# Which side of a trip through memory is cut in four: the store of the transposed probabilities, or the load

## The chip, the cores and the metric

The kernel runs on one core of one Trainium2 chip. The metric is device time in microseconds (us), the median over several executions. A profile of one execution shows its engines: PE (TensorE matrix products; PEld is its weight load), DVE (VectorE), ACT (ScalarE), POOL (GpSimd) and SP (SyncE, which here only issues transfers). Transfers (DMAs) issued by SP and ACT run on the same sixteen DMA engines.

## The reference, cut to what matters

Eight sequences of 512 rows of 256 numbers (float32) go through causal attention with 16 query heads in 4 groups, and then through a mixture of 64 experts with a shared expert. What matters here is the attention of one head:

```
scores = q @ k.T / sqrt(128)          # 512 x 512, query t by key s
scores = where(s <= t, scores, -inf)
probs  = softmax(scores, axis=-1)
out    = probs @ v                    # sum over keys s
```

The softmax is taken along the keys, so a row of probabilities has its query in the partition. The product with v sums over the keys, so TensorE wants the keys in the partition: each head's probabilities have to be transposed between the two.

## The kernel before, in words

There are 8 x 16 = 128 heads, numbered k, and one long loop over them (L944). The order of the instructions on each engine is written out by hand (`manual_schedule`, L135). An iteration k does, in this order:

- `scores(k, 0)` and `scores(k, 1)`: products of q and k, a DVE reduction that adds the mask and finds the maximum (L293), and the exponential on ACT (L296);
- `turned(k - 1)` (L312): the transposition of the head before;
- `scores(k, 2)` and `scores(k, 3)`; `weigh(k)`, in which POOL multiplies by the reciprocal sums (L306);
- `project(k - 3)`, `queries(k + 1)`, and `mix(k - 2)` (L343), which multiplies the transposed probabilities `et` with v (L349).

So what `turned(k)` makes in iteration k + 1 is used in iteration k + 2, after that iteration's scores, projection and queries.

`turned` works in two steps, because DVE's transpose works inside blocks of 32 x 32. First, six DVE transposes (L322) turn the blocks in place, into `eb`, which holds, for partition p, four chunks c (which block of 32 keys inside a tile of 128), each with ten blocks of 32 numbers (only the tiles on and below the diagonal). After that, partition p = 32 a + s of `eb` holds, in chunk c, numbers that belong in partition 32 c + s of `et`, chunk a. This exchange of the block index a with c goes through memory. `ex_d` is a scratch tensor in memory of 128 rows by 4 x 320 numbers, of which there are two, used in turn. One transfer stores `eb` to it as it is, 128 rows of 5,120 bytes (L326). Four transfers then load `et`, one for each 32 partitions c of it: each takes from 128 rows of `ex_d` a piece of 1,280 bytes (L329). All five are issued by SP, which takes its instructions strictly in order; the loads wait for the landing of the store. Each head has its own such trip, except the last two (126 and 127), which TensorE transposes (`turned_at_once`, L332).

There is one buffer `eb` (`bufs=1`, L314), so DVE's transposes of the next head wait until the store has read it. There are two buffers `et`, so the load for head k waits until `mix(k - 2)` is done.

Other transfers on SP stand around these: loads of the next sequence's rows `x`, stores of rows for the feed-forward part, and, late in the loop, the result. From about head 97 on the expert part runs inside the same loop: ACT issues three loads of 352 KB for each of 32 pairs of experts (L523, L530), between its exponentials, and POOL gathers and scatters rows. All transfers of SP and ACT use eight completion semaphores in turn, in the order of the program, and a transfer is issued only when the one eight places ahead of it has landed.

Of the kernel before, what the change touches and what calls it, by code (L numbers as in the profile page):

```python
# [22 lines left out]
NI = T // P  # L23
BS = 32
# [20 lines left out]
def sandwich_kernel(ctx, tc, x, wq, bq_t, wkv, bk_t, bv, wo, gate_wt, w_gate, w_up, w_down,  # L45
                    sh_gate_t, sh_up_t, sh_down_t, pe_t, out):
    nc = tc.nc
# [75 lines left out]
    with ExitStack() as part:  # L123
# [38 lines left out]
        for half, (t, w) in enumerate(((sg_sb, sh_gate_t), (su_sb, sh_up_t))):  # L162
            nc.sync.dma_start(out=t[:, :, :FSH], in_=w.rearrange("(c p) n -> p c n", p=P))
            nc.sync.dma_start(out=t[:, :, FSH:],
                              in_=gate_wt.rearrange("(c p) n -> p c n", p=P)[:, :, ts(half, NX // 2)])
# [146 lines left out]
        def turned(k):  # L312
            l = live[k]
            eb = p2.tile([P, NI, NB, BS], F32, tag="eb", name=f"eb_{k}", bufs=1)  # L314
            for i in range(NI):
                for js in ([0, 1], [2, 3]):
                    js = [j for j in js if j <= i]
                    if not js:
                        continue
                    at, step = AT[js[0]] + i - js[0], AT[js[-1]] - AT[js[0]] - 1  # L320
                    blocks = eb[:, :, at : at + step * (len(js) - 1) + 1 : max(step, 1), :]
                    nc.vector.transpose(  # L322
                        blocks.rearrange("p c j t -> p j c t"),
                        l["e"][i][:, js[0] * P : (js[-1] + 1) * P].rearrange("p (j c t) -> p j c t", c=NI, t=BS))
            ex = ex_d[k % 2]
            nc.sync.dma_start(out=ex, in_=eb.rearrange("p c n t -> p c (n t)"))  # L326
            l["et"] = p2.tile([P, NI, NB, BS], F32, tag="et", name=f"et_{k}")
            for c in range(NI):
                nc.sync.dma_start(out=l["et"][ts(c, BS)].rearrange("s a n t -> s a (n t)"),  # L329
                                  in_=ex[:, c, :].rearrange("(a s) f -> s a f", s=BS))  # L330

        def turned_at_once(k):  # L332

# [610 lines left out]
        for k in range(NK):  # L944
            b, s = divmod(k, NH)
# [3 lines left out]
            if 0 <= k - 1 < NK - 2:  # L949
                turned(k - 1)  # L950
# [141 lines left out]
```

## Time and profile before

| what | value |
|---|---|
| three runs | 1455.51, 1459.09, 1459.84 us; median 1459.09 |
| the profiled execution, its own time | 1456.37 us |
| span of its core | 1454.6 us, mean granted TensorE clock 0.987 |
| PE busy | 1403.1 us, 96% of the span |
| DVE, ACT, POOL busy | 892.8, 505.8, 429.2 us |
| DMA moved | 252.03 MB, mean 173 GB/s |
| issues `ex_d<-eb` (L326) | 126, 640 KB each |
| issues `et<-ex_d` (L329) | 504, 160 KB each |

The span runs from the core's first to its last instruction; the execution's own time is 1.8 us more. Busy time is a share of the span over all stages; what counts at a place is which wait ends last there. In the 40 slices of the span, a digit 9 is 90% or more. A group of instructions shows its busy time, the mean of one, and, after the bar, how long its engine stood idle just before and for what. In the list of waits, a line says which engine at which line waited for what, the sum in us, the number of waits and the longest. "SPq" is SP's queue, which is not counted as busy.

### The profile page before, as it was taken

To read this page: it belongs to the slowest core of one execution; us is meant where nothing else is said; L and a number is where in the kernel's file an instruction comes from. 1 tells how busy PE (TensorE), PEld (TensorE's weight loads), DVE (VectorE), ACT (ScalarE), POOL (GpSimd) and SP (SyncE) were. 2 spreads that over 40 slices of the span, in tenths; PEclk is the share of its full clock that TensorE was granted. 3 is DMA by queue.
4 is the path that set the end of the run, shared out by engine and by line. 5 is a ranking of instruction groups with operands and counts; after the bars stand their busy time and mean duration, and the time that the engine had idled before them with its cause. 6 is when DMAs were issued, how large, how long until landed. Compare 5 with 4: busy or idle time off the path is not lost. (4 is left out here: it accounts for less than half of the span.)

```text
span 1454.6 us, 18553 instructions
## 1 busy us (share of the span) xinstructions
PE 1403.1 (96%) x5310; PEld 855.2 (59%) x5310; DVE 892.8 (61%) x3097; ACT 505.8 (35%) x1442; POOL 429.2 (30%) x686
## 2 busy tenths in 40 slices
PE   9999999999999999999999999999989999999895
PEld 5665665656556665666566665655545655556563
DVE  5565576656765577557665676576455454567634
ACT  2333343234422333234323442233433243434431
POOL 2222232123211231124211321125434444344511
PEclk9999999999999999999999999999999999999998
DMA  7664464355544554445534554449999889878812
GB/s 258 195 201 141 144 181 146 95 156 167 164 128 128 163 174 128 122 145 182 155 109 139 165 173 128 123 139 264 258 261 234 230 241 260 220 196 235 248 53 81
DMA packets 160790, 252.03 MB, mean 173 GB/s; under 512 B 16412, under 2 KB 136189, under 8 KB 160685
## 3 DMA queue, kind: packets, MB, share of 16 engines
q1 hardware_dynamic: 125869, 201.52, 46.5%
q10 hardware_dynamic: 28672, 39.85, 9.9%
q0 software_dynamic: 6144, 9.44, 3.4%
q8 instruction: 44, 0.72, 0.2%
q14 instruction: 61, 0.50, 0.1%
HBM read 143.01 MB, written 107.74 MB: 172 GB/s over the span
## 5 line engine op out<-in xcount | busy, mean ns | idle before, releaser
L306 POOL TENSOR_SCALAR e<-e,recip 128x128 f32<-128x128 f32 x508 | 274.1, 597 | 787.0 <-DVE recip L303 749.1
L296 ACT ACTIVATE e<-e,least 128x128 f32<-128x128 f32 (+3 forms) x512 | 285.8, 559 | 377.5 <-DVE least L293 338.9
L289 PE MATMUL psc<-kt,qt 128*128 128x128 f32 (+3 forms) x1024 | 310.0, 442 | 13.9 <-DVE qt L279 6.7
L349 PE MATMUL pav<-et,v 128*128 128x512 f32 (+3 forms) x1024 | 300.0, 436 | 5.0 <-DMA et<-ex_d 3.4
L349 PEld LDWEIGHTS pav<-et,v 128*128 128x128 f32 x1024 | 194.9, 192 | 166.8 <-issue 122.6
L293 DVE CUSTOM_DVE_ANT_0 e<-psc,mask 128x128 f32<-128x128 f32 (+3 forms) x512 | 232.7, 479 | 74.9 <-PE psc L289 67.5
L361 PE MATMUL po<-wo_sb,ao 128*128 128x256 f32 x1024 | 243.5, 381 | 0.7 <-ACT ao L109 0.7
L276 PE MATMUL pq<-xnt,wq_sb 128*128 128x512 f32 x512 | 242.1, 595 | 0.0
L361 PEld LDWEIGHTS po<-wo_sb,ao 128*128 128x128 f32 x1024 | 193.0, 190 | 72.3 <-issue 40.7
L322 DVE STREAM_TRANSPOSE eb<-e 128x128 f32<-128x128 f32 x756 | 228.1, 365 | 8.6 <-DMA ex_d<-eb 6.4
L109 ACT COPY ao<-pav 128x512 f32<-128x512 f32 x128 | 74.9, 585 | 427.4 <-PE pav L349 406.7
L289 PEld LDWEIGHTS psc<-kt,qt 128*128 128x128 f32 x1024 | 167.9, 192 | 90.7 <-issue 22.2
L279 DVE SCALAR_TENSOR_TENSOR qt<-pq,bq_sb,pe_sb 128x512 f32<-128x512 f32 x128 | 95.5, 746 | 93.5 <-PE pq L276 93.3
L276 PEld LDWEIGHTS pq<-xnt,wq_sb 128*128 128x128 f32 x512 | 96.3, 191 | 69.7 <-issue 64.2
L303 DVE RECIPROCAL recip<-total 128x4 f32<-128x4 f32 x128 | 22.8, 178 | 121.6 <-ACT e L296 120.6
L296 ACT ACTIVATION_READ_ACCUMULATOR e<-e,least 128x1 f32 x512 | 95.8, 187 | 0.0
L586 POOL DMA_INDIRECT y_d<-dd,idx x32 | 51.2, 1600 | 130.3 <-DMA y_d<-dd,idx 85.6
L248 PE MATMUL pk<-xnt,wkv_sb 128*128 128x512 f32 x128 | 60.3, 594 | 0.2 <-ACT xnt L109 0.2
L261 DVE TENSOR_TENSOR v<-pv,bv_sb 128x512 f32<-128x512 f32 x32 | 22.1, 691 | 60.8 <-PE pv L259 60.8
L259 PE MATMUL pv<-wkv_sb,xnt 128*128 128x512 f32 x128 | 59.1, 593 | 0.0
L112 DVE COPY ht<-pth 88x256 f32<-88x256 f32 x32 | 13.4, 418 | 67.8 <-PE pth L566 52.9
L251 DVE SCALAR_TENSOR_TENSOR kt<-pk,bk_sb,pe_sb 128x512 f32<-128x512 f32 x32 | 24.0, 750 | 47.4 <-PE pk L248 47.4
(197 smaller groups left out, 1118.2 us busy)
## 6 DMA issues: line engine op xcount, KB each, us to landing
ex_d<-eb SPq DMA_DIRECT2D x126, 640.0 KB
et<-ex_d SPq DMA_DIRECT2D x504, 160.0 KB
wgu<-in_w_gate ACTq DMA_DIRECT2D x32, 352.0 KB
wgu<-in_w_up ACTq DMA_DIRECT2D x32, 352.0 KB
wd<-in_w_down ACTq DMA_DIRECT2D x32, 352.0 KB
y<-y_d ACTq DMA_DIRECT2D x10, 512.0 KB
x<-in_x SPq DMA_DIRECT2D x8, 512.0 KB
x_d<-x SPq DMA_DIRECT2D x8, 512.0 KB
```

What stands on the lines that cost most here:

```text
L109: nc.scalar.copy(dst, src)
L248: nc.tensor.matmul(pk, lhsT=wkv_sb[:, c, g, 0, :], rhs=s["xnt"][:, c, :], start=c == 0, stop=c == NC - 1)
L259: nc.tensor.matmul(pv, lhsT=s["xnt"][:, c, ts(i, P)], rhs=wkv_sb[:, c, :, 1, :], start=c == 0, stop=c == NC - 1)
L276: nc.tensor.matmul(pq, lhsT=wq_sb[h // QPG][:, c, ts(h % QPG, D)], rhs=seqs[b]["xnt"][:, c, :], start=c == 0, stop=c == NC - 1)
L279: nc.vector.scalar_tensor_tensor(qt, pq, bq_sb[:, h : h + 1], pe_sb, ALU.add, ALU.add)
L289: nc.tensor.matmul(psc[:, :w], lhsT=l["qt"][:, ts(i, P)], rhs=seqs[b]["kt"][h // QPG][:, :w], start=True, stop=True)
L293: nc.vector.tensor_tensor_reduce(out=e, in0=psc[:, :w], in1=mask[:, T - w :], scale=-1.0 / math.sqrt(D), scalar=BIG, op0=ALU.add, op1=ALU. ...
L296: nc.scalar.activation(e, e, AF.Exp, bias=l["least"][:, i : i + 1], scale=-1.0, accum_out=l["total"][:, i : i + 1])
L306: engine.tensor_scalar(e, e, recip[:, n : n + 1], 1.0, ALU.mult, ALU.mult)
L322: nc.vector.transpose(blocks.rearrange("p c j t -> p j c t"), l["e"][i][:, js[0] * P : (js[-1] + 1) * P].rearrange("p (j c t) -> p j c t", ...
L349: nc.tensor.matmul(pav[:, :, j:, :], lhsT=seqs[b]["v"][:, j, ts(g, D)], rhs=l["et"][:, :, AT[j] : AT[j] + NI - j, :], start=j == 0, stop=j ...
L361: nc.tensor.matmul(po[b][i // 2][:, i % 2, :], lhsT=ao[:, ts(i, P)], rhs=wo_sb[:, h, :], start=h == 0 and i % 2 == 0, stop=h == NH - 1, sk ...
```

## The change

The store is cut in four and the load is made whole. For each a, the 32 partitions 32 a to 32 a + 31 of `eb` are stored by one transfer; chunk c of partition 32 a + s goes, as a piece of 1,280 bytes, to row 32 c + s of `ex_d`, place a. So `ex_d` has the rows of the partitions of `et`, and one transfer loads them: 128 rows of 5,120 bytes. The bytes are the same, and there are five transfers as before, all on SP, in the same place of the program. The order of instructions on DVE, ACT, POOL and PE is the same; the semaphore waits around the transfers differ, and so does the place of some ACT loads between SP's transfers in the common order of the eight semaphores.

```diff
             ex = ex_d[k % 2]
-            nc.sync.dma_start(out=ex, in_=eb.rearrange("p c n t -> p c (n t)"))
+            for a in range(NI):
+                nc.sync.dma_start(out=ex[:, a, :].rearrange("(c s) f -> s c f", s=BS),
+                                  in_=eb[ts(a, BS)].rearrange("s c n t -> s c (n t)"))
             l["et"] = p2.tile([P, NI, NB, BS], F32, tag="et", name=f"et_{k}")
-            for c in range(NI):
-                nc.sync.dma_start(out=l["et"][ts(c, BS)].rearrange("s a n t -> s a (n t)"),
-                                  in_=ex[:, c, :].rearrange("(a s) f -> s a f", s=BS))
+            nc.sync.dma_start(out=l["et"].rearrange("s a n t -> s (a n t)"), in_=ex.rearrange("p a f -> p (a f)"))
```

## The prediction

> **What bounds the kernel now.** First the page's slices: who is busy, and where.
>
> ```profile
> PE   9999999999999999999999999999989999999895
> PEclk9999999999999999999999999999999999999998
> DMA  7664464355544554445534554449999889878812
> ```
>
> PE is full from start to end, while the DMA engines are half idle up to slice 27 and full behind it. A table by stage, with sum of PE in each, says how much is to be won:
>
> ```profile
> 27.00:980.00 953.00, 945.01 (x3295) 578.77 (x3294) 612.13 (x2129) 331.01 (x972) 232.83 (x429) 1.00 0.50 150
> 1000.00:1280.00 280.00, 269.04 (x1261) 156.16 (x1260) 152.01 (x523) 99.36 (x272) 124.61 (x142) 0.98 0.94 241
> 1280.00:1400.00 120.00, 109.13 (x420) 70.06 (x419) 77.79 (x273) 50.76 (x136) 48.14 (x70) 0.96 0.72 209
> ```
>
> Columns: stretch, its length, PE busy first, then the other engines, at the end the clock, the DMA share and GB/s. PE idles 8 us in 953 of the quiet stage, 11 in 280 of the expert stage, 11 in 120 of the tail. Now what of this the trip through memory causes: the groups that read `et` and write `eb`, and the waits of SP.
>
> ```profile
> L349 PE MATMUL pav<-et,v 128*128 128x512 f32 (+3 forms) x1024 | 300.0, 436 | 5.0 <-DMA et<-ex_d 3.4
> L322 DVE STREAM_TRANSPOSE eb<-e 128x128 f32<-128x128 f32 x756 | 228.1, 365 | 8.6 <-DMA ex_d<-eb 6.4
> SPq L326 <- DVE eb L322: 457.9, 105, 9.8
> SPq L329 <- DMA ex_d<-eb: 427.1, 125, 10.8
> ```
>
> PE stands 5.0 us before these 1024 products, 3.4 of it one wait for `et`; DVE stands 6.4 us for `eb` to be free. SP's 427 us for the store cost nothing as long as `et` is in time. So the trip is nearly all hidden, and the question is how near it is to showing. A quiet head on SP:
>
> ```profile
> 608.58 0.34 SPq L326 DMA_DIRECT2D ex_d<-eb  x1
> 611.58 1.73 SPq L329 DMA_DIRECT2D et<-ex_d  x4
> ```
>
> 3.00 us from store issue to first load issue. The trace's semaphore updates and packets give the rest (medians of 64 quiet heads). Store: first packet 0.84 us after issue, last packet ended at 2.59, landed at 2.94; its 128 packets of 5,120 bytes take 199 ns each, eight per engine, 1.59 us. Loads: issued 0.43 apart, so the fourth at 1.30; packets from 0.93 to 4.16, landed at 4.88; their 512 packets of 1,280 bytes take 84 ns in the mean, though the shortest take 53. Round trip 2.94 + 0.06 + 4.88 = 7.88 us. From landing to the first product of that head there are 4.0 us in the median of heads 0 to 79, at least 0.14; above 2 us in nearly all. From store landing to DVE's next transpose: mostly above 2.5 us, least 0.8 in the quiet stage.
>
> The only places where it shows are in the expert stage at 1049 and 1184 (PE gaps of 1.28 and 0.32 us before `pav`) and here, in the chain that ended last:
>
> ```profile
> 1356.31 5.21 DMA out_dram<-x
> 1361.54 0.38 SPq L670
> 1362.02 7.22 DMA ex_d<-eb
> 1370.63 3.63 DMA et<-ex_d
> 1374.39 4.60 PE pav L349 x8
> ```
>
> Head 124's store waits behind a result and an `x` load on SP, then shares the DMA with 1.5 MB of others, and PE waits 3.40 us for `et` at 1374.
>
> [...] Here the smallest undisturbed store, 128 KB of zeros at 24.81 us, landed after 1.97 us[...].
>
> **The change part by part.**
>
> *Removed:* one store (2.94 us to landing) and four loads (4.88). SP issue 0.34 + 4 x 0.43 = 2.1 us.
>
> *Added, the four stores.* The last is issued at 1.30 us. [...] 1.30 + 0.84 + eight packets of 55 ns (0.44) + 0.35 receipt = 2.93. If it is limited as the loads were (packets over 3.23 us): 0.84 + 3.23 + 0.35 = 4.42; with the loads' slower landing 4.88. I take 4.4[...]. A gain below 2.93 is excluded by the issue spacing.
>
> *Added, the one load.* 0.93 + 1.75 (the store's packet span[...]) + the loads' landing lag of 0.72 = 3.4; at worst 4.88 as now. The wait before it is for four or five semaphores instead of one: 0.06 becomes about 0.2 (where SP had more than one semaphore before a load it was 0.37).
>
> *Sum:* 4.4 + 0.2 + 3.4 = 8.0 us against 7.88. Ends: 2.93 + 0.06 + 3.4 = 6.4, and 4.88 + 0.37 + 4.88 = 10.1. So the round trip is mirrored, not shortened.
>
> *Quiet stage.* I laid the longer trip over the measured slack of each head, counting that a stall of PE gives the next head so much more slack: +0.5 us costs 0.5 us in heads 0 to 96 together, +1.0 costs 2.5, +2 costs 6.7, +3 costs 18. A shorter trip gains nothing, because PE works throughout: cover is PE's own 9.5 us or so per head. At +0.1: 0. DVE's next transposes see `eb` free 1.5 us later; in five quiet heads with margin 0.8 to 1.3 (where an `x` transfer stands ahead of the store) DVE stops some 0.5 us. Behind it are the reductions of the other two score tiles (1.4 us) and `qt`; PE has 1.9 us of projection, 1.9 of queries and 2.3 of `pav` before it needs `qt`. Nothing.
>
> *What is queued behind on SP.* The single load is issued at 4.4 + 0.2, done at 4.9; before, the fourth load was out at 3.0 + 1.73 = 4.73. Stores and loads behind it move by 0.2 us.
>
> *Expert stage.* Here the DMA is full (0.94). Store and loads take 4.6 to 11 and 5 to 13 us[...]. That too is mirrored: stores 3 us longer, load 3 us shorter. The et waits (1.28, 0.32) should go: -1.6. Two heads, at 1040 and 1062, have `eb` margins of 1.6 and 0.1, so DVE stops up to 3 us there; the second lies in a 4.28 us PE gap before `pd`, made by a late `wd`, which hides it. I count +1. The eight semaphores: the built program shows the first store of the head at 1049 (issued 9.3 us late because SP's queue stood behind its own loads) now waiting for one load rather than for two older loads, but its fourth store waits for `wd_late`, landed about 1052. Even: 0.
>
> *Tail.* Head 124's stores are bound by bytes (2.2 MB between 1360.5 and 1369.2), so they land at 1369.2 to 1370; then 0.2 + 3.4 instead of 5.0: -1.4 + 0.4 = -1.
>
> Total 0 - 1.6 + 1 - 1 = about -2 us: span 1453, own time 1454.5, and from the median of 1459.1 (the profiled execution was 2.7 below it) 1457. Measurement can tell about 0.3% (4.4 us) from nothing, so this is no change.
>
> **The rivals.**
>
> *Slower, by the single `eb`.* Stores of small packets in the full DMA land not 3 but 5 us later. The margins of `eb` in heads 99 to 113 (6.6, 5.2, 1.6, 0.1, 5.4, then mostly 4 to 12) are then short by 3.4, 4.9, 0.6 and 0.9, about 10 us, and DVE passes it to the scores. 1467. For it: the margin at 1060 is already gone. Against: PE's gap there has another cause. It decides from about 4 us on.
>
> *Slower, by the trip itself.* The four stores do not overlap as the loads did[...]: trip at the bound of 10.1 us or beyond, +2.5 to +3, 18 to 29 us over all heads: 1480. For it: nothing in the trace shows a store from 32 partitions. Against: loads of the same shape overlap.
>
> *Faster.* [...] trip at 6.4 in the quiet and 2 to 3 us less in the full stage, so weights land earlier: PE's gaps before `pd` (0.8, 4.3, 3.0) halve, and the tail wait of 3.4 mostly goes: -4 - 1.6 - 2.5 = -8: 1451. Against: the bytes are equal.
>
> **How the numbers follow.** No change 0.48, first rival 0.24, second 0.10, faster 0.18. Range 1449 to 1472: it takes in the faster case and the first rival and leaves out the second. The no-change case alone is 1454 to 1462. Chances: faster 0.18, same 0.48, slower 0.34.
>
> **What would show it.** Right: 5,120-byte packets now in the load, 1,280-byte in the store; store landing at 4.2 to 4.5 in the quiet, load 3.2 to 3.5; no PE wait before `pav` up to 980; at 1374 a shorter one. DVE's wait for `ex_d<-eb` rises from 6.4 to 8 to 12 us. Wrong if SP's wait before the load grows by over 3 us per head in the quiet, if `pav` gets waits in many heads, or if DVE's wait for `eb` passes 20 us.

## The result, and the profile after

The changed kernel takes 1445.34 us (median of 6, 1443.11 to 1448.56) where the one before took 1459.94 beside it: a ratio of 0.991, 95% interval 0.9894 to 0.9926. It is 14.6 us, or 0.9%, faster. The forecast was 1457 with a range of 1449 to 1472 and a chance of 0.18 for faster, so it missed, on the side that I had held least likely.

The slices of the page after:

```profile
PE   9999999999999999999999999998999999999895
...
PEclk9999999999999999999999999999999999999998
DMA  7765565355544564355544564447998779878712
```

Behind slice 27 the DMA row now holds sevens and eights among its nines, where it held four nines in a row. The table by stage of the changed kernel, with the same columns and stretches as before (PE busy first after the length; at the end clock, DMA share, GB/s):

```profile
27.00:980.00 953.00, 945.01 (x3295) 578.75 (x3294) 613.00 (x2136) 332.00 (x976) 231.44 (x426) 1.00 0.54 150
1000.00:1280.00 280.00, 274.96 (x1287) 159.45 (x1286) 160.50 (x550) 103.55 (x282) 131.81 (x149) 0.99 0.87 247
1280.00:1400.00 120.00, 109.44 (x434) 69.28 (x433) 78.85 (x273) 49.97 (x132) 45.85 (x67) 1.00 0.64 199
```

The quiet stage is unchanged for PE to the hundredth: busy 945.01 of 953 us in both. In the expert stage PE is busy for 275.0 of 280 us instead of 269.0, and the DMA engines move more (247 GB/s, 241 before) while being busy less (0.87, 0.94 before). There the same bytes cost less DMA time (3.88 us per MB before, 3.48 after; the table of all forms below). In the quiet stage it is the other way: 150 GB/s in both, at a share of 0.54 instead of 0.50, which costs PE nothing.

The groups and SP's waits that the prediction had shown, after:

```profile
L349 PE MATMUL pav<-et,v 128*128 128x512 f32 (+3 forms) x1024 | 297.1, 433 | 4.0 <-DMA et<-ex_d 3.4
...
L322 DVE STREAM_TRANSPOSE eb<-e 128x128 f32<-128x128 f32 x756 | 227.5, 364 | 8.4 <-DMA ex_d<-eb 4.2
```

```profile
SPq L327 <- DVE eb L322: 485.4, 108, 10.0
SPq L330 <- DMA ex_d<-eb: 327.1, 216, 5.6
```

Little has changed in the sums at `et` and `eb`: 4.0 us instead of 5.0, 8.4 instead of 8.6. (The wait for four stores appears as several, 216 in number.) DVE's part is hidden by a label. Transfers share semaphores (829 of SP and ACT take eight in turn), and the profile names the transfer that it finds at the semaphore last:

```profile
DVE eb L322 <- DMA ex_d<-eb: 4.2, 2, 3.4
DVE eb L322 <- DMA wgu<-in_w_gate: 3.9, 1, 3.9
```

The second line is a wait for `eb` too. Its semaphores are those of one head's four stores, the last of which landed at 1059.44 us, and DVE went on at 1059.52. So DVE stood 8.1 us for the store, where it had stood 6.4.

The gain shows in what PE waited for between 1000 and 1300 us. First before, then after:

```profile
PE pd L575 <- DMA wd<-in_w_down: 8.3, 4, 4.3
PE psc L289 <- DVE qt L279: 2.1, 1, 2.1
PE pav L349 <- DMA wgu_late<-in_w_gate: 1.3, 1, 1.3
```

```profile
PE pgu L549 <- DVE hid L559: 1.4, 1, 1.4
PE pq L276 <- ACT sc L388: 0.9, 1, 0.9
PE pgu L549 <- DVE gs L716: 0.6, 1, 0.6
PE pd L575 <- DMA wd<-in_w_down: 0.5, 1, 0.5
```

The 1.3 us before `pav` are, in spite of their label, a wait for the trip: their semaphores include those of the four loads of `et`, the fourth of which landed at 1050.01 us, 12 us after its issue. After the change PE has no wait for `et` in this stage. That is the part of the trip itself, and it is small. The expert product `pd` waited 8.3 us for its weights `wd`, and now waits 0.5. That load is issued by ACT, is not touched by the change, and lands 7.4 us after issue in the median instead of 9.0. From the first score to the last product of the expert part behind the loop's end the trace has 1408.8 us instead of 1421.5; PE's gaps between 1000 and 1300 us fall from 13.1 to 5.5 us, and PE's busy time from 1403.1 to 1397.9, with the mean granted clock at 0.993 instead of 0.987. So of the 12.7 us between the two spans 7.6 are gaps, and the rest goes with shorter PE busy time at a higher granted clock. Why the clock was higher was not tested.

In the quiet the trip is nearly what the prediction said it would be. SP's queue in the changed kernel, the same head as was shown before:

```profile
609.96 1.86 SPq L327 DMA_DIRECT2D ex_d<-eb  x4
614.23 0.34 SPq L330 DMA_DIRECT2D et<-ex_d  x1
```

4.27 us from the first store's issue to the load's, and by the landing records (medians of 68 quiet heads) 4.19 us for the stores, 4.01 for the load: 8.3 us for the trip, 7.9 before.

In the expert stage it is not: there the stores were to land 3 us later and the load 3 us earlier. By the same records (medians of heads 99 to 115) the one store took 6.6 us and the four take 6.7; the four loads took 10.2, and the one takes 6.5. The trip fell from 16.8 us to 13.2.

### The profile page after: what moved, and what is told of

It is laid out like the page before. It is cut to its first block, busy times and chain, and to the rows that moved or that the text cites. A ratio compares the mean times of both kernels' runs of the same rounds, so it can differ in the third digit from the quotient of the medians.

```text
span 1443.4 us, 18558 instructions
## 1 busy us (share of the span) xinstructions
PE 1397.9 (97%) x5310; PEld 851.9 (59%) x5310; DVE 893.8 (62%) x3097; ACT 506.5 (35%) x1442; POOL 430.2 (30%) x686
## 4 chain that ended last, share of the span: by engine, by line
PE 78%; DVE 13%; ACT 3%; DMA 2%; issue 2%; POOL 0%; ACTq 0%; SPq 0%; DVEq 0%; POOLq 0%
PE psc L289 16%; PE pav L349 16%; PE pq L276 12%; PE po L361 12%; PE pk L248 4%; PE pv L259 4%; DVE eb L322 4%; ACT e L296 3%; PE psg L703 3%; PE psu L703 2%; PE pgu L549 2%; PE py L730 2%; PE pd L575 2%; DMA ex_d<-eb 1%; DVE e L293 1%
## 5 line engine op out<-in xcount | busy, mean ns | idle before, releaser
L306 POOL TENSOR_SCALAR e<-e,recip 128x128 f32<-128x128 f32 x508 | 269.6, 554 | 819.3 <-DVE recip L303 780.6
```

The costliest lines, as they stand in the source:

```text
L306: engine.tensor_scalar(e, e, recip[:, n : n + 1], 1.0, ALU.mult, ALU.mult)
```

## The experiments

Four theories stood after the result. *Ports* (a name and no more, since no view shows a port): the old load writes into a quarter of the partitions at a time, and this holds up the weight loads that run beside it. *Pieces*: small pieces in the load are the cost, whatever the partitions. *Order*: one store and four loads, or four and one, stand differently in the common order of the eight semaphores, so ACT's loads are issued at another time. *Trip*: the trip itself is what is late. Each ratio below is to the kernel before, timed beside the run in question; its median lay between 1455.6 and 1459.9 us.

**Where it arises: the changed form in a part of the heads.** Both kernels compute the full result.

```diff
+            new = 97 <= k < 117        # stage_not: not 97 <= k < 117
+            if new:
+                (four stores, one load, as after)
+            else:
+                (one store, four loads, as before)
```

> The changed form for heads 97 to 116 alone (the expert stage), the old form for all others. If the whole gain arises in the expert stage, as the two traces say (PE gaps of 12.1 us there before, 3.8 after), the time is 1445 to 1449 us. If part of it arises in the quiet heads or the tail, it is 1450 to 1456.

> The reverse: the old form for heads 97 to 116, the changed form elsewhere. If the gain is of the expert stage, 1457 to 1461 us; if the quiet heads or the tail share in it, 1450 to 1456.

With the change in 20 heads alone: 1443.9 us, ratio 0.9904 (0.9875 to 0.9934). With it in the other 106: 1459.6, ratio 1.0013 (0.9995 to 1.0032). The first lies 1.1 us under its forecast, the second inside. All of the gain is of the expert stage, and the longer trip in the quiet costs nothing that can be measured.

**Partitions or pieces: the old order with another load.** Here and in all kernels below marked `_z` the exchange of blocks is left out, so `et` holds the blocks in wrong places.

```diff
 # loads128: a quarter of each row, into all partitions
-                nc.sync.dma_start(out=l["et"][ts(c, BS)].rearrange("s a n t -> s a (n t)"),
-                                  in_=ex[:, c, :].rearrange("(a s) f -> s a f", s=BS))
+                nc.sync.dma_start(out=l["et"][:, c].rearrange("s n t -> s (n t)"), in_=ex[:, c, :])
 # loads32big: whole rows, into a quarter of the partitions
+                nc.sync.dma_start(out=l["et"][ts(c, BS)].rearrange("s a n t -> s a (n t)"), in_=ex[ts(c, BS)])
```

> One whole store and four loads as before, but each load takes 1,280 bytes into all 128 partitions instead of four pieces of 1,280 into 32. The exchange of blocks is left out, so et holds the blocks in the wrong place; counts, bytes and piece sizes are those of before. Ports theory (writing a quarter of the partitions at a time holds up the weight loads): 1443 to 1450 us, weights' 1,408-byte packets near 70 ns as after (81 before). Pieces theory (small pieces in the load are the cost, whatever the partitions): 1456 to 1461. Order theory (one store then four loads keeps the semaphores of ACT's loads busy longer): 1456 to 1461.

> One whole store and four loads into 32 partitions each as before, but each partition takes one row of 5,120 bytes. The exchange of blocks is left out; the order of all transfers and semaphores is exactly that of before. Ports theory: still slow, 1455 to 1461 us. Pieces theory: 1443 to 1450. Order theory: 1456 to 1461.

Both totals, 1500.5 and 1521.3 us, miss all expectations. The profile says why: behind the loop, both ran one extra pass over an expert pair, because the wrong blocks changed what the router chose. Up to that pass the trace does answer: first score to last product of the expert part is 1401.8 us with all partitions (before 1421.5) and 1422.0 with whole rows into a quarter of them. Small pieces are not the cost: the kernel with small pieces into all partitions is fast, the one with large pieces into a quarter is slow, like before. To have the totals too, the next kernels hold the number of extra passes at zero.

```diff
-            nc.vector.tensor_scalar(lst[:, 0:1], lst[:, 0:1], -1.0, 0.0, ALU.add, ALU.max)
+            nc.vector.tensor_scalar(lst[:, 0:1], lst[:, 0:1], -1000.0, 0.0, ALU.add, ALU.max)
```

> The kernel of loads128 again (whole store, four loads of 1,280 bytes into all partitions, the exchange of blocks left out), with the number of extra expert passes at the end set to zero, as it is with the true data; with the wrong blocks the router had asked for one pass of some 78 us. Ports theory, from the profile of loads128 up to that pass (first score to last product 1401.8 us, after 1408.8, before 1421.5): 1436 to 1442 us. If the total does not follow the profile, 1450 to 1460.

1438.0 us, ratio 0.9882 (0.9865 to 0.9898), inside the interval of the ports theory. The extra pass had cost 1500.5 - 1438.0 = 62.5 us, and without as much loads32big would stand at about 1458.8, where before stands; that total is worked out, not run.

**The other side: the stores, and the floor.**

```diff
 # stores128_z: a quarter of each row, from all partitions; whole load
+                nc.sync.dma_start(out=ex[:, a, :], in_=eb[:, a].rearrange("p n t -> p (n t)"))
 # stores32big_z: whole rows, from a quarter of the partitions; whole load
+                nc.sync.dma_start(out=ex[ts(a, BS)], in_=eb[ts(a, BS)].rearrange("s c n t -> s c (n t)"))
 # whole_both_z: one whole store, one whole load
```

> Four stores of 1,280 bytes from all 128 partitions and one whole load; exchange left out, extra passes zero. It asks whether reading a quarter of the partitions at a time costs anything that is left in the changed kernel. [...] 1434 to 1441 us. If only writing into SBUF matters: 1443 to 1448, as after.

> Four stores from 32 partitions each, as rows of 5,120 bytes, and one whole load; exchange left out, extra passes zero; the order of all transfers and semaphores is exactly that of after. If the small pieces of the stores cost something: 1435 to 1441 us. [...] 1443 to 1448.

> One whole store and one whole load, exchange left out, extra passes zero: two transfers instead of five. The floor for any form of the trip. Ports theory: near loads128_z, 1432 to 1441 us. Order theory: with three fewer semaphores taken per head, ACT's loads are issued earlier and it is far below, under 1430.

1439.5, 1444.7 and 1441.3 us; ratios 0.9886 (0.9869 to 0.9902), 0.9925 (0.9901 to 0.9949) and 0.9896 (0.988 to 0.9913). These intervals overlap or touch, and the totals do not separate the three well. The two forms that read a quarter of the partitions, stores32big_z and the changed kernel, stand at 1445, the two that read all at 1440; so something up to 5 us may be left on the store, which is not settled. By the forecasts (1434 to 1441 us if the partitions cost something in reading, 1435 to 1441 if the pieces do, 1443 to 1448 if neither), stores128_z speaks for a cost of the partitions in reading, and stores32big_z against a cost of the pieces. The trip in the quiet shows the first plainly: pieces of 1,280 bytes take 81 ns in the changed kernel and 56 when they are stored from all 128 partitions, and the four stores land after 4.19 and 3.26 us. Whole rows from 32 partitions (stores32big_z) land after 4.0, so it is the partitions and not the pieces. In the totals it is small beside the load's side. The floor with only two transfers, whole_both_z, lies at the upper edge of the ports theory's interval (1441.3, forecast 1432 to 1441), which speaks against the order theory: that had wanted it under 1430.

**Through what: no weight loads.** Both kernels leave out the loads for expert pairs 2 to 31, which then compute with the weights of pairs 0 and 1.

```diff
+            if key != "late" and m >= 2:
+                l["wgu"] = pairs["w"][m % 2]["wgu"]
+                return
```

(and the same for `wd`.)

> The kernel before without the loads of weights for expert pairs 2 to 31 (90 loads of 352 KB on ACT's queue); those pairs compute with the weights of pairs 0 and 1. If the trip's old load costs time because it holds up the weight loads, this runs as fast as the changed kernel without weight loads, within 4 us, and has no PE gap before pd. If the trip itself is what is late (et, eb, SP), it stays 9 us or more behind that kernel.

> The changed kernel without the same 90 weight loads. 1430 to 1440 us under both theories; what counts is the distance to before_noweights.

1441.5 and 1439.5 us, ratios to before of 0.9874 (0.9839 to 0.991) and 0.9865 (0.9829 to 0.9902): 2 us apart, where 14.6 were. The stage of each, 1000 to 1280 us; first the old form without weight loads, then the new one:

```profile
1000.00:1280.00 280.00, 278.01 (x1312) 161.62 (x1312) 164.22 (x563) 107.05 (x288) 134.10 (x153) 1.00 0.56 141
```

```profile
1000.00:1280.00 280.00, 278.01 (x1310) 162.31 (x1310) 164.19 (x564) 106.54 (x288) 133.78 (x153) 1.00 0.56 141
```

PE is busy 278.01 us in both and the clock is 1.00. Taking the weight loads away from the old kernel wins 18 us, more than the change did. The gain of the change needs the weight loads beside the trip. Which of the two is late does not follow from this pair alone, since the trip is quicker too without them: in heads 99 to 115 the old load takes 4.9 us instead of 10.2. That is decided by the waits shown above. PE stood 8.3 us for `wd` and 1.3 for `et`, so the trip theory holds for a small part at most. What the change removes is mainly a disturbance of the weight loads: `wd` lands after 7.4 us instead of 9.0.

**Partitions or order: two loads.** One gap was left. The kernels before and loads32big have the same common order of SP's and ACT's transfers, and both need the longer time; all forms that gain had another. So a pair was run in which counts and bytes are the same, and the order too but for 22 of 595 places. (The pieces differ, 5,120 and 2,560 bytes; loads128 and loads32big have shown that small pieces are not what costs.)

```diff
 # loads64_z: two loads of whole rows, 64 partitions each
+                nc.sync.dma_start(out=l["et"][ts(c, 2 * BS)].rearrange("s a n t -> s (a n t)"),
+                                  in_=ex[ts(c, 2 * BS)].rearrange("p a f -> p (a f)"))
 # loads2x128_z: two loads of half rows, all partitions
+                nc.sync.dma_start(out=l["et"][:, ts(c, 2)].rearrange("s a n t -> s (a n t)"),
+                                  in_=ex[:, ts(c, 2), :].rearrange("p a f -> p (a f)"))
```

> One whole store and two loads of 320 KB, each into 64 partitions as rows of 5,120 bytes; exchange left out, extra passes zero. Ports theory[...]: as slow as four loads into 32, 1452 to 1460 us, weights' 2,048-byte packets near 130 ns. Order theory (the semaphore order of one store and four loads is the cost): fast like the whole load, 1438 to 1445, since this order is another one.

> The same, but each of the two loads takes half of every row (2,560 bytes) into all 128 partitions. Counts and bytes are equal to those of loads64_z, and the common order of SP's and ACT's transfers is the same but for 22 of 595 places. Ports theory: 1437 to 1443 us, weights' 2,048-byte packets near 113 ns. Order theory: equal to loads64_z within 4 us.

1456.6 us, ratio 0.9997 (0.9981 to 1.0012), and 1433.9, ratio 0.9832 (0.9803 to 0.9861). A load into 64 partitions is no better than into 32, as the forecast of the ports theory had it, though nothing had shown it before; the same bytes cut along the row have the lowest total of all, 3 us under the ports theory's interval. loads64_z leaves the exchange out like the `_z` kernels that gain, and gains nothing, so leaving it out is not where their gain comes from. The waits of PE from 1000 to 1300 us, first with 64 partitions, then with 128:

```profile
PE pd L574 <- DMA wd<-in_w_down: 7.3, 4, 4.3
PE psc L289 <- DVE qt L279: 3.7, 2, 2.4
PE pgu L548 <- DVE gs L715: 2.9, 1, 2.9
```

```profile
PE pgu L548 <- DVE gs L715: 1.7, 1, 1.7
PE psc L289 <- DVE qt L279: 1.0, 2, 0.9
PE pd L574 <- DMA wd<-in_w_down: 0.5, 2, 0.3
```

The 7.3 us for `wd` is the mark of the kernel before (8.3), the 0.5 that of the kernel after. And the same stretch by engine, 64 partitions, then 128:

```profile
1000.00:1300.00 300.00, 284.25 (x1311) 165.85 (x1310) 164.28 (x566) 106.40 (x288) 133.39 (x153) 0.98 0.91 240
```

```profile
1000.00:1300.00 300.00, 294.97 (x1368) 172.66 (x1367) 176.53 (x601) 114.45 (x313) 137.90 (x159) 1.00 0.84 249
```

More bytes at a lower share, and 10.7 us more of PE in 300. The order theory, which wanted the two equal, falls.

A relative of it can be looked up in the traces. A load of the trip that lands late keeps its semaphore longer, so ACT could be held at its next weight load. The time that ACT stood idle just ahead of a weight load, until the load's semaphore came free, sums to 16.1 us before the change and 3.1 after. But loads64_z, which gains nothing, has 3.5, and loads128_z, which gains, has 12.2: this holding is not what tells the two groups apart.

All forms side by side, from the packet records of the traces between 1000 and 1260 us. Packet means are of the weights `wd` (2,048 bytes on ACT's queue); DMA time is the sum of all packets' time over 16 engines, per MB moved; the span runs from the first score to the start of the last product of the expert part behind the loop.

| kernel | load into | `wd` packet, ns | DMA us per MB | `wd` landing, us | span, us |
|---|---|---|---|---|---|
| before | 32 at a time | 132 | 3.88 | 9.0 | 1421.5 |
| loads32big | 32 | 128 | 3.78 | 8.8 | 1422.0 |
| loads64_z | 64 | 132 | 3.81 | 9.4 | 1422.6 |
| after | 128, whole | 109 | 3.48 | 7.4 | 1408.8 |
| stores32big_z | 128, whole | 115 | 3.44 | 7.6 | 1407.2 |
| stores128_z | 128, whole | 116 | 3.43 | 6.7 | 1408.6 |
| whole_both_z | 128, whole | 112 | 3.40 | 7.6 | 1406.4 |
| loads128_z | 128, in four | 115 | 3.44 | 6.4 | 1398.8 |
| loads2x128_z | 128, in two | 117 | 3.43 | 7.2 | 1398.9 |

The kernels fall into two groups by one property of the load, how many partitions a load writes at a time: 3.78 to 3.88 us per MB where it is 32 or 64, 3.40 to 3.48 where it is 128. Why loads128_z and loads2x128_z have some 8 us less again is visible in part: in both, the tail wait of 3.4 us before `pav` is gone.

**Towards a faster version.** What is left in the changed kernel's tail is head 124. The chain of its end:

```profile
1353.81 0.49 SPq L327
...
1354.35 5.51 DMA ex_d<-eb
...
1360.08 1.81 DVE eb L322 x6
```

```profile
SPq L670 <- DMA out_dram<-x: 4.5, 1, 4.5
```

Its stores are still held on SP behind a load (L670) that waits for a result, and PE stands 3.44 us before `pav`. Two edits went at that; both compute the full result.

```diff
 # te124: heads 124 and 125 on TensorE
-            if 0 <= k - 1 < NK - 2:
+            if 0 <= k - 1 < NK - 4:
-            if k == NK - 1:
+            if k >= NK - 3:
 # late_step: the extra finishing step behind the next head's stores
-            if finishing and s in (12, 14):
+            if finishing and s in (13, 15):      # placed after turned(k - 1)
```

> The changed kernel with heads 124 and 125 transposed on TensorE like the last two, so that the wait of 3.4 us before pav at the end of the loop goes. It costs PE some 1.1 us per head. 1441 to 1446 us, if the wait does not move elsewhere.

> The changed kernel with the extra finishing step of iterations 124 and 126 moved behind the stores of the next head's trip, so that SP does not hold these behind a load that waits for a result to land. The 3.4 us wait before pav should shrink to under 1: 1440 to 1445 us. If DVE's or POOL's part of the step becomes late instead: no gain.

1444.3 us, ratio 0.9905 (0.9869 to 0.9942), and 1445.5, ratio 0.9914 (0.9884 to 0.9943): no gain over the changed kernel. In te124 the `pav` wait is gone, but gaps of 1.75 us before the new transposes and 1.06 before scores take its place; in late_step the `pav` wait is gone too, and gaps of 1.33 before scores and 2.5 before the last heads' transposes have come. The wait moved elsewhere. No version with the full result beats the changed kernel by a measurable amount.

## Why the prediction was wrong

*The trip in the quiet* was right within half a microsecond: stores 4.4 forecast and 4.19 measured, load 3.4 and 4.01, sum with the wait 8.0 and 8.3. The 4.4 for the stores was an estimate that carried the 3.23 us of the old loads' packets over to them; it came near, and the cost of the 32 partitions is now measured: 81 ns per piece from 32 partitions, 56 from all 128 (stores128_z). The lower end, 2.93, is the sum without such a cost, and "receipt" in it stands for the 0.35 us from the end of the last packet (2.59) to the landing (2.94). The load lies outside the 3.2 to 3.5 us that were named as a sign, because its 5,120-byte packets take 256 ns in the middle of the quiet heads and not the store's 199. Of the excess of the old loads' packets, 84 ns against a shortest of 53, only about half goes with the number of partitions: the same pieces into all 128 partitions take 69 ns in the quiet (loads128_z). And the 1.97 us of the store of 128 KB at 24.81 are 0.60 us to its first packet, 1.00 of packets and 0.37 from there to its landing.

*The quiet stage at zero* was right: stage_not measured 1.0013 (0.9995 to 1.0032), and PE's busy time in the stage is the same.

*DVE's wait for `eb`* was forecast to rise to 8 to 12 us, and it rose to 8.1. As forecast, the margins at 1040 and 1062 ran out (0.80 and 3.93 us of waiting), and the fourth store there waited for `wd_late`, until 1051.56. PE's gap of 1.4 us before `pgu` follows from it, where +1 had been counted.

*The waits for `et`* were counted at -1.6. The 1.28 went. The 0.32 at 1184 stayed (0.33 after), for it was never a wait for `et`: its only semaphore is ACT's.

*The tail* was forecast at -1 and gave nothing: the `pav` wait at head 124 is 3.44 us instead of 3.40.

*The expert stage* is the step that failed, in two places. The first is "That too is mirrored: stores 3 us longer, load 3 us shorter." The load became 3.7 us shorter, but the stores took 6.7 us where they had taken 6.6. The sentence carries the quiet stage's exchange over to the full one and takes the DMA time there as given by the bytes. It is not: a MB costs 3.88 us in the old form and 3.48 in the new, a tenth less, and the packets of `wd`, which the change does not touch, fell from 132 ns to 109. The second is the sentence on the 4.28 us gap before `pd`, "made by a late `wd`, which hides it". I had the true bottleneck in sight, used it as a cover for another wait, and did not ask why `wd` was late. So the sum had no term for the weight loads. The waits of `pd` were 8.3 us, the largest PE wait of the stage, and 7.8 of them went.

The rival *faster* named a shorter trip in the full stage and earlier weights, and forecast that the gaps before `pd` would halve. For the full stage it was right in kind and too small: 8 us where 14.6 came. The gaps before `pd` went almost wholly (8.3 to 0.5), while the tail, for which it had reckoned 2.5 us, gave nothing; and the shorter PE busy time (5.2 us) was in no sum. Its trip of 6.4 us in the quiet was wrong (8.3). It was given 0.18 with the argument "the bytes are equal", which is no argument on what those bytes cost the transfers beside them. A cost of the 32 partitions was reckoned in the prediction for the latency of the trip alone, not for its neighbours.

The totals go with the number of partitions: two loads into 64 take 0.9997 of before, which loads into 32, and two loads into 128 take 0.9832. By what way the writing of few partitions holds up the weights, and why 64 are no better than 32, no view shows. Shown is that the number of partitions that a load writes at a time makes the difference, and PE's waits (8.3 us for `wd` before, 0.5 after) and the weights' packets (132 ns, then 109) show that it acts mainly through the weight loads.

## What to carry to other kernels

When a transfer has to be cut and runs beside other loads in a stage where the DMA is full (a share of 0.94 here), try the form in which each load writes all 128 partitions (here 3.40 to 3.48 us of DMA per MB, against 3.78 to 3.88 with 32 or 64), and put the cut that goes by partitions on the store (in the full stage 64 ns a piece from 32 partitions, 58 from 128). In this kernel next to nothing was to be won in the transfer itself (1.3 us of PE's waits for `et`); the gain lay in the loads of others that run beside it. So look for the longest wait on a DMA in that stage, and compare the mean time of that transfer's packets with the shortest of their size (for `wd` 132 ns against 81) before a neighbour of it is priced at nothing. Where a gap is used as a cover for something, ask first what made it. And where transfers share semaphores, check a wait's label against what the instruction can be waiting for.

## What was not expected of the hardware

The two directions differ, and so do the two stages. Mean times of a piece of 1,280 bytes, from the packets of SP's queue (quiet: median over the heads 0 to 79; full: 1000 to 1260 us; the shortest is 53 ns throughout):

| piece of 1,280 bytes | quiet stage, ns | full stage, ns |
|---|---|---|
| loaded into 32 partitions (before) | 84 | 98 |
| loaded into 128 (loads128_z) | 69 | 72 |
| stored from 32 (after) | 81 | 64 |
| stored from 128 (stores128_z) | 56 | 58 |

What 32 partitions cost a load grows from the quiet stage to the full one, from 15 ns to 26; what they cost a store shrinks, from 25 to 6. Why is not known. And cutting a load in two along the row was no dearer than one load: loads2x128_z, with three transfers, took 1433.9 us, and whole_both_z with two 1441.3.
